# An mLSTM layer in a four-layer kernel: source order for two more engines in its first pass, row work and output norm spread over more chunks

## The chip, the cores and the metric

One core of a Trainium2 chip runs the whole program. Its engines are TensorE (PE, whose weight loads are listed apart as PEld), VectorE (DVE), ScalarE (ACT), GpSimd (POOL) and SyncE (SP); here SP and ScalarE start the DMAs. The metric is the device time of one execution in microseconds (us), lower is better. All times below are us where nothing else is said.

## The reference

Eight images of 32 x 32 positions and 256 channels, in fp32, pass through four residual layers, each `x = x + L_i(groupnorm(x))`. Layers 0, 2 and 3 are attention layers and don't change. Layer 1 is an mLSTM over the 1024 positions of an image, with 8 heads of 64:

```python
up = xs @ W_up.T                                  # 256 -> 1024
x_m, z = up[..., :512], up[..., 512:]
x_act = silu(conv_b + causal_conv4(x_m))          # 4 taps along the sequence
q, k = block_diag(x_act); v = block_diag(x_m)     # 4 x 4 blocks
ig, fg = gates(q, k, v)                           # 8 rows each
lc = cumsum(log_sigmoid(fg))
logD = where(tril, lc_i - lc_j + ig_j, -inf)
m = max_j(logD); D = exp(logD - m)
C = (q @ k.T / 8) * D
h = (C / (max(|sum_j C|, exp(-m)) + 1e-6)) @ v
hn = layernorm_per_head(h) * norm_w
out = ((hn + skip * x_act) * silu(z)) @ W_down.T
```

## The kernel before, in words

All four layers are in one program. Layer 1 is the function `layer1` (from L776). It cuts each image into two segments of 512 tokens, 16 in all, channels on the partitions and tokens in the free dimension, and makes two passes over them.

**First pass** (L1117 to L1160): 64 units u = 4s + c, s the segment and c a quarter of the 512 inner channels. A unit projects `x_m` for its quarter (four matmuls with the z half, `up`, L845), copies it (ScalarE, L864), convolves (ScalarE's tap L871, then three on VectorE, L876) in a bank of PSUM, and takes two Silus (`silu_a` of two units before, L882; `silu_z`, L889). `xm` carries three tokens of the segment before; POOL copies them (L861). When a segment is done its `xm`, `xa` (x_act) and `sz` (silu of z) go to DRAM, and `gates` (L894) makes its gate rows, also for DRAM. In an odd segment the next image's group norm is computed (`norm`, steps stats, mean, scale; `normed` applies it on POOL), the image itself having been asked for one image earlier (`load_x`, on ScalarE's DMA queue).

**Row work** (`rows`, L923 to L1000): for a group of four images, 32 rows (image, head) of 1024 tokens. It is eleven pieces: fetch, soft (|f| and min), soft2 (Exp and Ln, the log-sigmoid), sums (a scan along the row, VectorE), a, most (a second scan), before, within, low, exps (three Exps) and turned (transposes on TensorE into `cols`). Row results that the second pass wants go to DRAM. Group 0's pieces run in the first pass, one a unit from u = 36; group 1's ("late") in the second, at chunks 0, 1, 2, 2, 3, 3, 4, 4, 5, 6 and 7 of their list.

**Second pass** (L1161 to the end): 64 chunks of 128 tokens, four a segment and eight an image; the state is new at each image's first chunk. In chunk n:
- `maxima` (L1045) fetches the row maxima for chunk n+3 into the buffer `d`; `masked` (POOL, L1051) subtracts them from the causal mask for chunk n+2; `decays` (ScalarE, L1056) exponentiates d for chunk n+1 in two halves.
- `scores` (L1176): 8 matmuls into two banks, and VectorE multiplies them into d (L1191).
- for chunk n+1: `queries` (`g`, copied by ScalarE L1077; `gr` = g times the row factor `rb`, VectorE L1080), `keys` (`xt` transposed, weighted into `xaw`, L1092), `value` (`vt`, copied by ScalarE L1106).
- `within` (L1193): the row sums `sums` and the numerators `num_ps`; `across` (L1213) adds the part from the state, then ScalarE evacuates `num_ps` twice (copy L1238, square L1239).
- `update` (L1246): `kv_ps` on TensorE; the old state times its decay on POOL (`decayed`, L1270) and VectorE's sum (L1274, L1276) make the new state.
- Units of the segment before: `spread_rows` (ScalarE's square L1281, `var_ps` L1286, an add on VectorE, ScalarE's Ln L1290 and Exp L1291) in the segment's first chunk; `finish` 0 and 1 (`bc_ps` on TensorE L1297, four operations on VectorE L1301 and L1302, two multiplies on POOL L1305) both in the second; `down` 0 and 1 (L1310, the residual add, the store to DRAM) in the fourth. After the last chunk, four rounds of these remain.

Buffers: the ring of PSUM banks "m" has 4 banks in the first pass (beside 4 for the convolution) and 7 in the second (beside `sums`); every PSUM tile comes from it in turn, so an unread tile holds up the seventh request after it. `d` has four buffers.

**What orders the work.** Inside `manual_schedule` the named engines run their instructions in source order. In the first pass that holds for TensorE and ScalarE; VectorE, POOL and SP are ordered by a scheduler. In the second pass it holds for all but SP. ScalarE's functions come in sets that a table load exchanges; `preload_act_table_set` (L944, L982, L1165) asks for the set that has both Ln and Exp. `start` (L1111) asks for the second pass's first data and masks, at u = 58.

Of the kernel before, what the change touches and what calls it, by code (L numbers as in the profile page):

```python
# [16 lines left out]
P = 128  # L17
# [4 lines left out]
HALF = 512  # L22
# [402 lines left out]
def image_parts(x):  # L425
    return [[x[:, c, hs] for _, hs in halves()] for c in range(2)]
# [349 lines left out]
def layer1(tc, K, src, dst, n_img, a, first):  # L776
# [4 lines left out]
    with tc.tile_pool(name="l1w", bufs=1, reuse_waits="tile") as wk, tc.tile_pool(  # L781
# [41 lines left out]
        def norm(b, step):  # L823
            if step == 0:
                gn.stats(b, image_parts(x[b]))
            elif step == 1:
                gn.mean(b)
            else:
                gn.scale(b)

        def normed(s):
            for c in range(2):
                gn.apply(nc.gpsimd, s // 2, c, seg(s)[:, c], seg(s)[:, c])
# [89 lines left out]
        def rows(i, temp):  # L923
# [18 lines left out]
            def soft2():  # L942
                sp = q["sp"]
                nc.scalar.preload_act_table_set("natural_log_exp_and_others")  # L944
                nc.scalar.activation(sp, sp, AF.Exp, scale=-1.0)
                nc.scalar.activation(sp, sp, AF.Ln, bias=epsn[0:NR, 1:2])
# [34 lines left out]
            def exps():  # L981
                nc.scalar.preload_act_table_set("natural_log_exp_and_others")  # L982
                for k in ("sp", "f", "lc"):
                    nc.scalar.activation(q[k], q[k], AF.Exp)
                nc.sync.dma_start(rowd[i][1], q["sp"])
                nc.sync.dma_start(rowd[i][2], q["lc"])
# [16 lines left out]
        rb, xv, g, gr, xaw, dt, num, sq, nrow = ({} for _ in range(9))  # L1003
# [41 lines left out]
        def maxima(n):  # L1045
            b, t = divmod(n, 2 * NCH)
            dt[n] = wk.tile([P, 4, 2, P], F32, name="d", bufs=4)
            r8 = 8 * (b % GRP)
            r = rowd[b // GRP][0][r8 : r8 + 1, t * P : (t + 1) * P]
            nc.sync.dma_start(dt[n], bass.AP(r.tensor, r.offset, [[0, P], [L, 8], [1, P]]))  # L1050
# [60 lines left out]
        def start():  # L1111

            load_x(0)
            load(0)
            for n in range(3):
                maxima(n)
            masked(0)  # L1117
            masked(1)

        with tc.tile_pool(  # L1120
            name="l1p", bufs=1, space=PSUM, reuse_waits="tile"
        ) as pp, tc.tile_pool(
            name="l1g", bufs=1, space=PSUM, reuse_waits="tile"
        ) as gp, tc.manual_schedule(engines={E.PE, E.Activation}):
            banks["m"] = pp, 4
            if n_img > 1:
                load_x(1, True)
            units = {}
            for i in range(NG - 1):
                todo = rows(i, lambda: wk.tile([P, 2, L], F32, tag="num", name="row", bufs=2))  # L1130
                for k, f in enumerate(todo):
                    units.setdefault(8 * GRP * (i + 1) + 4 + k, []).append(f)
            for u in range(4 * NS + 3):
                s, c = divmod(u, 4)
                if s < NS:
                    b = s // 2 + 1
                    if s % 2 == 0 and c == 0 and s and b < n_img:
                        load_x(b)
                    project(s, c)
                    convolve(s, c)  # L1140
                    if s % 2 and b < n_img and c < 3:
                        norm(b, c)
                    if s % 2 and b < n_img and c == 3:
                        normed(s + 1)
                    if s and s % 2 == 0 and c == 1:
                        normed(s + 1)
                if u >= 2 and u - 2 < 4 * NS:
                    silu_a(*divmod(u - 2, 4))
                if u < 4 * NS:
                    silu_z(s, c)  # L1150
                if NG > 1 and u == 4 * NS - 6:
                    start()
                if NG > 1 and u == 4 * NS + 2:
                    queries(0)
                    keys(0)
                    value(0)
                if c == 2 and s:
                    gates(s - 1)
                for f in units.get(u, []):
                    f()  # L1160
        with tc.tile_pool(  # L1161
# [3 lines left out]
            nc.scalar.preload_act_table_set("natural_log_exp_and_others")  # L1165
            late = rows(NG - 1, lambda: K.big("row"))
            if NG == 1:
                for f in late:
                    f()
                start()  # L1170
                queries(0)
                keys(0)
                value(0)
                late = []
            at = (0, 1, 2, 2, 3, 3, 4, 4, 5, 6, 7)
            late = {n: [f for m, f in zip(at, late) if m == n] for n in range(2 * NCH)}  # L1176
# [68 lines left out]

            def update(n):  # L1246
# [21 lines left out]
                dc = wk.tile([P, 4, 130], F32, name="decayed")  # L1268
                e = rb[s][:, :, t * P + P - 1 : t * P + P].to_broadcast([P, 4, 130])
                nc.gpsimd.tensor_mul(dc, states[n % 2], e)  # L1270
# [8 lines left out]
            def spread_rows(s):  # L1279
                r = nrow[s]  # L1280
                nc.scalar.activation(  # L1281
                    r, r, AF.Square, bias=epsn[:, 0:1], scale=math.sqrt(1e-5)
                )
                ps = ring("var_ps")
                for c in range(4):
                    nc.tensor.matmul(  # L1286
                        ps[32 * c : 32 * c + 32], sel, sq[s][:, c], start=True, stop=True
                    )
                nc.vector.tensor_add(r, r, ps)
                nc.scalar.activation(r, r, AF.Ln)  # L1290
                nc.scalar.activation(r, r, AF.Exp, scale=-0.5)  # L1291

            def finish(s, i):
                ps = [ring("bc_ps") for _ in range(2)]
                for j in range(2):
                    r = slice(64 * i + 32 * j, 64 * i + 32 * j + 32)
                    nc.tensor.matmul(ps[j], bcw[r], nrow[s][r], start=True, stop=True)  # L1297
                for j in range(2):
                    c = 2 * i + j
                    h = num[s, "s"][:, c]  # L1300
                    nc.vector.tensor_mul(ps[j], h, ps[j])  # L1301
                    nc.vector.scalar_tensor_tensor(  # L1302
                        h, xa[s][:, c], par[:, c, 5:6], ps[j], ALU.mult, ALU.add
                    )
                    nc.gpsimd.tensor_mul(h, h, sz[s][:, c])  # L1305

            def down(s, m):
                ps = ring("dn_ps")
                for c in range(4):
                    nc.tensor.matmul(  # L1310
                        ps, wdn[:, c, m * P : (m + 1) * P], num[s, "s"][:, c],
                        start=c == 0, stop=c == 3,
                    )
                nc.vector.tensor_add(seg(s)[:, m], seg(s)[:, m], ps)
                if m == 1:
                    nc.sync.dma_start(dst[:, :, s * HALF : (s + 1) * HALF], seg(s))

            def units(n, k):

                s, t = divmod(n, NCH)  # L1320
                s -= 1
                if s < 0:
                    return
                at = 3 * t + k
                if at == 1:
                    spread_rows(s)
                elif at in (3, 5):
                    finish(s, (at - 3) // 2)
                elif at in (9, 10):
                    down(s, at - 9)  # L1330
# [17 lines left out]
            def prefetch(n):  # L1348
                s, t = divmod(n, NCH)
                if n and n % (2 * NCH) == 0:  # L1350
                    load_x(s // 2)
                if t == 0 and s + 1 < NS:
                    load(s + 1)
                    load_rb(s + 1)
                if t == 3 and s < NS:
                    load_z(s)

            load_rb(0)
            decays(0, range(4))
            for n in range(N):  # L1360
                prefetch(n)
                if n + 3 < N:
                    maxima(n + 3)
# [4 lines left out]
                if n + 1 < N:  # L1368
                    decays(n + 1, (0, 1))
                    keys(n + 1)  # L1370
                    value(n + 1)
                units(n, 1)
# [5 lines left out]
                update(n)  # L1378
                if n + 2 < N:
                    masked(n + 2)  # L1380
                for f in late.get(n, []):
                    f()
                if K.next:
                    follow(N - n)
            for n in range(N, N + NCH):
                for k in range(3):
                    units(n, k)
# [942 lines left out]
```

## Time and profile before

| | us |
|---|---|
| median of 3 runs | 3371.83 (3370.86 to 3379.88) |
| profiled execution | 3368.94 |
| its span | 3367.2 |
| layer 1, first `up` matmul to layer 2's first matmul | 1090.0 to 2026.6 |
| its first pass | 1090.0 to 1370.2 |
| its second pass, image 0 | 1370.2 to 1462.4 |
| its second pass, the other images | 1462.4 to 1998.5 |
| from the last scores to layer 2 | 1998.5 to 2026.6 |
| mean granted clock of TensorE in the span | 0.974 |

The trace shows an engine's instructions in groups: start, duration, engine and line, the operation, out<-in by the program's names, partitions x elements, count. Brackets at the end are the idle time of the engine in front of the group and what ended it. `ACT_TABLE_LOAD` is ScalarE's change of table set. The granted clock is a share of full speed.

Matmul records of the layer's largest groups: `up_ps` x512 takes 232.4, `dn_ps` 116.4, `num_ps` 75.3 for the part inside the chunk and 62.6 from the state, `sc` 74.4, `g_ps` 74.0, `vt_ps` 68.6. On ScalarE `decays` (L1062) takes 164.0 in 512 instructions of 392 ns; on POOL `masked` 152.4 in 64 of 2386 ns; on VectorE d times scores 81.9 in 128 of 681 ns.

### The profile page before, as it was taken

The numbers are of one execution on the slowest core, as the hardware profiler recorded it, in microseconds if no ns is written. First come the engines' busy times: TensorE is split into PE (matmuls) and PEld (weight loads), VectorE is DVE, ScalarE is ACT, GpSimd is POOL, SyncE is SP. The second block draws the span as 40 slices with busy tenths as digits, with TensorE's granted clock in tenths as the row PEclk, the third lists the DMA queues.
The fourth block names the chain that finished last, engine by engine and source line by source line (L and its number), as shares of the span: only waits on it lengthen the run. The fifth ranks groups of instructions, "written<-read, shape, count | busy, mean of one in ns | idle before, by whom it ended". The sixth has DMA issues, their size and how long they took to land.

```text
span 3367.2 us, 77570 instructions
## 1 busy us (share of the span) xinstructions
PE 3206.9 (95%) x30760; PEld 1646.7 (49%) x30760; DVE 2177.8 (65%) x5559; ACT 2247.9 (67%) x5040; POOL 1490.2 (44%) x1069
## 2 busy tenths in 40 slices
PE   7999999999998998899999989999998999999997
PEld 3323323323222444666666755666664555555554
DVE  4776776776675666555555565666665667777775
ACT  3666666766666668554554446667776788889885
POOL 4233233223321011244444445343435667888777
PEclk9999999999999999999999999999999779999999
DMA  3000000000001666767777733111111001111001
GB/s 139 14 26 1 26 26 1 26 17 11 26 7 39 240 225 217 231 182 181 195 194 184 211 91 101 46 58 52 40 49 48 14 14 33 32 34 39 27 27 61
DMA packets 138911, 268.00 MB, mean 80 GB/s; under 512 B 9202, under 2 KB 77172, under 8 KB 130228
## 3 DMA queue, kind: packets, MB, share of 16 engines
q1 hardware_dynamic: 132164, 242.67, 23.7%
q10 hardware_dynamic: 6384, 20.37, 1.9%
q8 instruction: 243, 3.98, 0.5%
q14 instruction: 120, 0.98, 0.1%
HBM read 177.81 MB, written 85.20 MB: 78 GB/s over the span
## 4 chain that ended last, share of the span: by engine, by line
PE 71%; ACT 9%; DVE 6%; POOL 6%; issue 4%; DMA 3%; POOLq 0%; ACTq 0%; SPq 0%; DVEq 0%
PE s L675 7%; PE sm L693 6%; PE num L720 6%; PE qkv_ps L1763 5%; PE qkv_ps L1982 4%; PE dn_ps L1310 3%; PE up_ps L849 3%; PE qk_ps L550 3%; PE pt L1545 3%; PE pt L1673 2%; PE fac_ps L2084 2%; ACT e L2043 2%; PE o_ps L603 2%; PE pr_ps L1823 2%; PE o L1564 2%
## 5 line engine op out<-in xcount | busy, mean ns | idle before, releaser
L681 DVE TENSOR_TENSOR e<-s,ret 128x1024 f32<-128x1024 f32 x512 | 602.9, 1219 | 180.5 <-PE s L675 176.5
L685 ACT ACTIVATE ea<-e 128x1024 f32<-128x1024 f32 x512 | 535.1, 1054 | 268.1 <-DVE e L681 234.1
L675 PE MATMUL s<-qk,qk 32*128 32x512 f32 x2048 | 300.5, 640 | 2.4 <-POOL qk L567 1.7
L1531 POOL TENSOR_TENSOR e<-e,su 128x616 f32<-128x616 f32 (+2 forms) x128 | 157.3, 1229 | 270.3 <-DVE su L1530 239.2
L693 PE MATMUL sm<-ea,ones 128*32 128x512 f32 x2048 | 273.0, 604 | 2.0 <-DVE dn L701 2.0
L720 PE MATMUL num<-e,v 128*32 128x512 f32 x2048 | 266.6, 592 | 0.0
L1678 DVE COPY pts<-pt 112x512 f32<-112x512 f32 x256 | 175.9, 687 | 133.9 <-PE pt L1673 132.4
L2043 ACT ACTIVATE e<-win,disc 128x196 f32<-128x196 f32 x512 | 239.6, 544 | 0.2
L849 PE MATMUL up_ps<-x,wup 128*128 128x512 f32 x512 | 232.4, 606 | 4.8 <-ACT sz L889 2.3
L1663 POOL TENSOR_TENSOR e<-e,su 128x784 f32<-128x784 f32 x128 | 191.4, 1495 | 87.1 <-DVE su L1662 59.8
L1655 ACT ACTIVATE e<-e,mx 128x196 f32<-128x196 f32 x512 | 228.0, 453 | 0.0
L2050 POOL TENSOR_TENSOR e<-e,win 128x784 f32<-128x784 f32 x128 | 201.8, 1577 | 38.1 <-issue 31.5
L1526 ACT ACTIVATE e<-e,mx 128x154 f32<-128x154 f32 (+2 forms) x512 | 212.1, 425 | 0.0
L1053 POOL TENSOR_TENSOR d<-cmask,d 128x1024 f32<-128x1024 f32 x64 | 152.4, 2386 | 105.7 <-DMA d<-l1rows 105.7
L1982 PE MATMUL qkv_ps<-xq,w 128*128 128x512 f32 x384 | 192.0, 627 | 1.2 <-ACT fac L2077 1.2
L1062 ACT ACTIVATE d<-d,cols 128x128 f32<-128x128 f32 x512 | 164.0, 392 | 43.3 <-POOL d L1053 43.2
L1763 PE MATMUL qkv_ps<-x,w 128*128 128x512 f32 x384 | 181.3, 609 | 1.6 <-POOL x L236 1.6
L1673 PEld LDWEIGHTS pt<-idg,e 128*112 128x112 f32 x1024 | 120.5, 139 | 121.1 <-issue 89.9
L675 PEld LDWEIGHTS s<-qk,qk 32*128 32x128 f32 x2048 | 85.3, 183 | 184.2 <-issue 119.1
L1305 POOL TENSOR_TENSOR num<-num,sz 128x512 f32<-128x512 f32 x64 | 81.4, 1272 | 207.6 <-ACT vt L1106 109.6
L1673 PE MATMUL pt<-idg,e 128*112 128x128 f32 x1024 | 165.1, 287 | 8.4 <-DVE oT L1697 3.1
L876 DVE SCALAR_TENSOR_TENSOR cv<-xm,par,cv 128x512 f32<-128x512 f32 x192 | 140.7, 750 | 47.0 <-ACT cv L871 44.1
(243 smaller groups left out, 6711.7 us busy)
## 6 DMA issues: line engine op xcount, KB each, us to landing
d<-l1rows SPq DMA_DIRECT2D x64, 512.0 KB
x<-x SPq DMA_DIRECT2D x25, 1024.0 KB
x<-x SPq DMA_DIRECT2D x32, 512.0 KB
l1xm<-xm SPq DMA_DIRECT2D x16, 1024.0 KB
l1sz<-sz SPq DMA_DIRECT2D x16, 1024.0 KB
xv<-l1xm SPq DMA_DIRECT2D x32, 512.0 KB
l1xa<-xa SPq DMA_DIRECT2D x16, 1024.0 KB
xa<-l1xa SPq DMA_DIRECT2D x16, 1024.0 KB
```

The lines of the kernel that those rows point to most:

```text
L675: nc.tensor.matmul(s[:, j % 2], qk[b, 1, c][g, kb * P : (kb + 1) * P], qk[b, 0, c][g, h * HALF : (h + 1) * HALF], start=True, stop=True,)
L681: nc.vector.tensor_mul(e[n, i], s, m)
L685: nc.scalar.activation(ea[n, i], e[n, i], AF.Abs)
L693: nc.tensor.matmul(acc["sm"][g, :], ones, ea[n, j // 2][:, j % 2, :], start=kb == 0, stop=kb == 7,)
L720: nc.tensor.matmul(acc["num"][g, :], v[b][:, kb, vc], e[n, j // 2][:, j % 2, :], start=kb == 0, stop=kb == 7,)
L849: nc.tensor.matmul(ps, wup[:, kc, m * P : (m + 1) * P], seg(s)[:, kc], start=kc == 0, stop=kc == 1,)
L1526: self.nc.scalar.activation(p[:, j], p[:, j], AF.Exp, scale=-1.0, bias=mx[:, j : j + 1], accum_out=su[:, j : j + 1],)
L1655: self.nc.scalar.activation(e[:, j], e[:, j], AF.Exp, scale=-1.0, bias=mx[:, j : j + 1], accum_out=self.su[:, j : j + 1],)
L1673: self.nc.tensor.transpose(ps[: self.PART, at : at + P], self.tile(n)[:, 2 * i + j, k * self.PART : (k + 1) * self.PART], self.K.ident,)
L1763: nc.tensor.matmul(ps, w[:, kc, o : o + P], x[b][:, kc, h * HALF : (h + 1) * HALF], start=kc == 0, stop=kc == 1,)
L1982: nc.tensor.matmul(ps, w[:, kc, o : o + P], xq[b][:, kc, h * HALF : (h + 1) * HALF], start=kc == 0, stop=kc == 1,)
L2043: nc.scalar.activation(e[:, j], win[:, 0], AF.Tanh, scale=disc[b][:, i, 8 + h : 9 + h], bias=disc[b][:, i, h : h + 1],)
```

## The change

It changes `layer1` alone.

1. In the first pass VectorE and POOL join TensorE and ScalarE in source order. The group norm's steps are placed by unit: for image b (first unit 8b) a quarter of `stats` in each of the units 8b−10 to 8b−7, `mean` at 8b−5, `root` at 8b−4, the two halves of `normed` at 8b−2 and 8b+1. Images from 2 on are asked for at 8b−16, two images ahead; every third has its own buffer.
2. Group 0's row pieces stand at u = 36 + (0, 2, 4, 5, 7, 8, 10, 12, 14, 16, 18). The late ones stand at chunks 0, 3, 4, ... 12, one a chunk, in front of `units(n, 1)` and `within`, where they stood at the chunk's end. The late pieces no longer ask for a table set; one request stands at the second pass's start, as before.
3. `start` stays at u = 58 without its masks; `load_rb(0)` moves from the second pass to u = 63, and the masks of chunks 0 and 1 to u = 63 and 65. `maxima` runs four chunks ahead, with five buffers for d.
4. `decayed` for chunk n+1 is computed at the end of chunk n, in front of `masked(n+2)` (`decay`).
5. Output norm: `squared` and `spread_rows` in the segment's first chunk, `finish` 0 in the second, `finish` 1 in the third, `down` in the fourth. The last segment goes in two halves of 256 tokens.
6. The second pass's `load_x` moves from an image's first chunk to its sixth, from the second image on.

```diff
-        ) as gp, tc.manual_schedule(engines={E.PE, E.Activation}):
+        ) as gp, tc.manual_schedule(engines={E.PE, E.Activation, E.DVE, E.Pool}):
...
+            for b in range(1, n_img):
+                u = 8 * b
+                if b > 1:
+                    at(u - 16, load_x, b, b % 3 == 1)
+                for i in range(4):
+                    at(max(u - 10, 1) + i, lambda b=b, i=i: gn.stats(b, image_parts(x[b]), i))
+                at(max(u - 5, 5), gn.mean, b)
+                at(max(u - 4, 6), gn.root, b)
+                at(max(u - 2, 7), normed, 2 * b)
+                at(u + 1, normed, 2 * b + 1)
...
-                for k, f in enumerate(todo):
-                    units.setdefault(8 * GRP * (i + 1) + 4 + k, []).append(f)
+                for k, f in zip((0, 2, 4, 5, 7, 8, 10, 12, 14, 16, 18), todo):
+                    at(8 * GRP * (i + 1) + 4 + k, f)
+            if NG > 1:
+                at(4 * NS - 6, start)
+                at(4 * NS - 1, load_rb, 0)
+                for i in range(2):
+                    at(4 * NS - 1 + 2 * i, masked, i)
+                for f in (queries, keys, value):
+                    at(4 * NS + 2, f, 0)
...
-            nc.scalar.preload_act_table_set("natural_log_exp_and_others")
-            late = rows(NG - 1, lambda: K.big("row"))
+            log_exp()
+            late = rows(NG - 1, lambda: K.big("row"), lambda: None)
...
-            at = (0, 1, 2, 2, 3, 3, 4, 4, 5, 6, 7)
-            late = {n: [f for m, f in zip(at, late) if m == n] for n in range(2 * NCH)}
+            late = dict(zip((0, 3, 4, 5, 6, 7, 8, 9, 10, 11, 12), late))
...
+            def decay(n):
+
+                if 0 < n % (2 * NCH) < 2 * NCH - 1:
+                    s, t = n // NCH, n % NCH
+                    decayed[n] = wk.tile([P, 4, 130], F32, name="decayed")
+                    e = rb[s][:, :, t * P + P - 1 : t * P + P].to_broadcast([P, 4, 130])
+                    nc.gpsimd.tensor_mul(decayed[n], states[n % 2], e)
...
+            for s in range(NS - 1):
+                n, w = NCH * (s + 1), slice(0, HALF)
+                at(n, 0, squared, s, w)
+                at(n, 1, spread_rows, s, w)
+                at(n + 1, 0, finish, s, 0, w)
+                at(n + 2, 0, finish, s, 1, w)
+                at(n + 3, 0, down, s, 0, w)
+                at(n + 3, 1, down, s, 1, w)
+            s, w = NS - 1, [slice(0, 2 * P), slice(2 * P, HALF)]
+            at(N - 2, 1, squared, s, w[0])
+            at(N - 2, 2, spread_rows, s, w[0])
+            at(N - 1, 2, finish, s, 0, w[0])
+            for f, *args in (
+                (squared, w[1]), (finish, 1, w[0]), (spread_rows, w[1]),
+                (down, 0, w[0]), (down, 1, w[0]), (finish, 0, w[1]), (finish, 1, w[1]),
+                (down, 0, w[1]), (down, 1, w[1]),
+            ):
+                at(N, 0, f, s, *args)
...
-                if n and n % (2 * NCH) == 0:
+                if n > 2 * NCH and n % (2 * NCH) == 5:
                     load_x(s // 2)
...
-            load_rb(0)
             decays(0, range(4))
             for n in range(N):
+                if n + 4 < N:
+                    maxima(n + 4)
                 prefetch(n)
-                if n + 3 < N:
-                    maxima(n + 3)
                 scores(n)
...
+                if n in late:
+                    late[n]()
                 units(n, 1)
                 within(n)
...
                 update(n)
+                decay(n + 1)
                 if n + 2 < N:
                     masked(n + 2)
-                for f in late.get(n, []):
-                    f()
```

## The prediction

> **What bounds the kernel now.** I read the page first (busy shares, then the chain that ended last), then the layer's four stages in the table of windows, then the groups of each engine inside one segment.
>
> ```profile
> PE 3206.9 (95%) x30760; PEld 1646.7 (49%) x30760; DVE 2177.8 (65%) x5559; ACT 2247.9 (67%) x5040; POOL 1490.2 (44%) x1069
> ...
> PE 71%; ACT 9%; DVE 6%; POOL 6%; issue 4%; DMA 3%; POOLq 0%; ACTq 0%; SPq 0%; DVEq 0%
> ```
>
> TensorE is busy 95% of the span and carries 71% of the chain. The changed layer can only win back TensorE's idle time, and the half-speed stretches that such idle time leaves behind. The stages of the layer (us; then busy time of PE, PEld, DVE, ACT, POOL; clock; DMA share):
>
> ```profile
> 1090.00:1370.20 280.20, 266.12 (x1601) 129.81 (x1599) 178.28 (x314) 188.59 (x293) 35.32 (x53) 0.98 0.65 234
> 1370.20:1462.40 92.20, 73.74 (x868) 56.69 (x868) 48.02 (x78) 47.78 (x108) 33.80 (x18) 0.89 0.73 193
> 1462.40:1998.50 536.10, 509.17 (x6088) 371.61 (x6087) 307.46 (x569) 273.38 (x701) 238.17 (x152) 0.99 0.69 180
> ```
>
> They are the first pass, the head of the second pass (chunks 0 to 7, image 0) and its other 56 chunks. Against each I set what TensorE alone needs.
>
> First pass: a clean segment (1330.18 to 1346.18) takes 15.85 of matmuls, so 16 take 254; seven group-norm steps at 0.5, the column transposes 1.1 and the last 2.3 make 260. It takes 280: **20 are lost**.
>
> Head: two clean segments are 63.85. It takes 92.2: **28.4 lost**, at a clock of 0.89.
>
> Rest: a clean segment is 36.5 where an image's first half is computed (no state yet) and 37.25 where its second half is, so 14 make 503.5 with the longer `sums`. It takes 536: **32.5 lost**. The lost time has a face here, VectorE's line of the same chunk first:
>
> ```profile
> 1599.07 0.85 DVE L1274 TENSOR_TENSOR state<-decayed,kv_ps 64x256 f32<-64x256 f32 x2 [1.61 <-POOL decayed L1270]
> ```
> ```profile
> 1600.84 0.94 PE L1204 MATMUL sums<-d,hot 128*32 128x128 f32 x16 [2.03 <-DVE d L1191]
> 1601.71 1.98 PE L1210 MATMUL num_ps<-d,vt 128*64 128x128 f32 x16
> ```
>
> Brackets hold the wait before a group and what ended it. Once a segment, in its third chunk, TensorE waits for `d*scores`; that is late because the chunk before gave VectorE two `finish` (8 operations, 5.8) and put their four POOL multiplies ahead of `decayed`, which the state add waits for. In four of seven cases the 2.03 wait is followed by half-speed matmuls (1.98, where the same group took 1.09 ten us earlier); every other segment waits 1.59, and is never slow after it.
>
> **Part 1, decay a chunk ahead and `finish` in two chunks.** No work is added (POOL 1.06, four VectorE operations 2.9, only moved). `decayed(n+1)` follows chunk n's state add, and each chunk has one `finish`. VectorE's largest chunk load falls by 2.9, more than the 2.03 wait, so the 14 stalls (25.9 with their small variation), the half-speed matmuls (about 1.6 in four segments) and most of the longer `sums` go: 32.5 if nothing comes in their place. `masked(n+2)` now stands behind `decayed` on POOL, whose 1.06 is costed below.
>
> **Part 2, a new cost on ScalarE.** The late row pieces no longer request the set that holds both Ln and Exp, and the remaining request ends, in the built order, at the program's very start. The second pass then runs on separate sets: each segment's Ln and Exp (of `nrow`) need a load each, 34 loads where there were 3. The trace prices one:
>
> ```profile
> 1299.07 1.28 ACT L1062 ACT_TABLE_LOAD   x1
> 1300.36 0.40 ACT L1062 ACTIVATE d<-d,cols 128x128 f32<-128x128 f32 x1
> ```
>
> 1.28 a load, and the next ACTIVATE starts 0.01 after its end. The Trainium skill, "ScalarE: Activation LUTs", "What ACT_TABLE_LOAD costs", gives 1283 ns plus a drain of 1380 ns, 2.66 a switch. By the rule 34 loads are 90 and a pair is 5.3; by the rows 43.6 and 2.57. I take the rows. ScalarE is busy only 273 of 536, so the sum of loads costs nothing by itself; the place does:
>
> ```profile
> 1583.02 0.72 ACT L1281 ACTIVATE nrow<-nrow,epsn 128x512 f32<-128x512 f32 x1
> 1584.49 0.63 ACT L1290 ACTIVATE nrow<-nrow 128x512 f32<-128x512 f32 x1 [0.75 <-DVE nrow L1289]
> 1585.15 0.63 ACT L1291 ACTIVATE nrow<-nrow 128x512 f32<-128x512 f32 x1
> 1585.69 1.26 ACT L1062 ACTIVATE d<-d,cols 128x128 f32<-128x128 f32 x4
> 1586.86 0.56 ACT L1238 COPY num<-num_ps 128x512 f32<-128x512 f32 x1
> 1587.32 0.59 ACT L1239 ACTIVATE sq<-num_ps 128x512 f32<-128x512 f32 x1
> ```
>
> This is a segment's first chunk; its first score matmul began at T = 1578.54. ScalarE's order stays: behind Ln and Exp stand four decays and the two evacuations of `num_ps`. `squared` ends at T+5.1 (its wait for VectorE then falls inside the first load); load, Ln, load, Exp add 1.28 + 0.63 + 1.28 + 0.63: `nrow` is ready at T+8.95. Four decays and two evacuations (2.2 with their overlaps) free the bank of `num_ps` at T+11.15. TensorE, in a chunk without state (6.44 of matmuls, then the next scores 1.09 and queries 1.09), wants `nrow` for the broadcast `bc` at T+8.62: 0.35 to 0.4 of wait. After it come `bc` 1.06 and `xt` 0.44, and `vt`, the seventh bank on, wants `num_ps`' own at T+10.5: 0.65. Together 1.05. With state, `decayed` puts the mask later on POOL (state at T+1.3, 1.06, mask 2.35: T+4.85), the decays behind it wait, and the chain moves by 1.4: 0.45 at `bc`, 1.15 at `xt`: 1.6. Seven of each: 18.6. Bounds: zero if the loads are wholly covered, 14 x 2.57 = 36 if nothing covers it, plus 1.6 in each segment whose wait reaches the 2.0 after which matmuls ran at half speed. Here the skill ("TensorE: Matmul & The Clock Gate", Part 1, the HAM clock gate) puts the fall at an idle window of about 3.4. By that rule no wait here would slow anything; by the rows a 2.03 wait did in four of seven. I keep the rows: waits of 1.05 and 1.6 stay under it. Gain of parts 1 and 2 together: 32.5 − 18.6 = **14** (−10 to 30).
>
> **Part 3, head.** Two things make it: `rb` (11.18 on VectorE, 5.59 on TensorE) and the row pieces, several to a chunk (TensorE waits 3.77 and, 34 later, 5.42).
>
> ```profile
> 1383.87 0.69 DVE L1080 TENSOR_TENSOR gr<-g_ps,rb 128x512 f32<-128x512 f32 x1 [11.18 <-DMA rb<-l1rows]
> ```
> ```profile
> 1407.89 1.16 PE L1204 MATMUL sums<-d,hot 128*32 128x128 f32 x16 [3.77 <-DVE d L1191]
> ```
>
> `load_rb(0)` is asked for five units earlier, but it reuses an `xm` buffer and stands on SP's queue behind the last segment's stores, which the last `silu_z` releases about when the second pass begins: 0 to 4 remain. One piece a chunk, the longest a scan of 2.3 to 3.0 on VectorE, fits the 8 of a chunk where pairs (two scans and row steps of 1.2) did not. Left: a load and two activations on ScalarE in chunk 3 or 4 (about 4, and 1.5 of slow clock), `rb` 3, small ones 1.5: 10 in place of 28.4. Gain **18** (12 to 24). The row fetch's DMAs go ahead of the fifth `d` on SP's queue; that is in the low end.
>
> **Part 4, first pass.** POOL and VectorE follow the source, and the masks move from u=58 to u=63 and 65.
>
> ```profile
> 1275.09 2.34 POOL L1053 TENSOR_TENSOR d<-cmask,d 128x1024 f32<-128x1024 f32 x1 [25.31 <-DMA d<-l1rows]
> ...
> 1277.61 0.78 ACT L871 ACTIVATE cv<-xm,par 128x512 f32<-128x512 f32 x1 [5.86 <-POOL xm L861]
> ```
>
> POOL waited 25.31 for a DMA with the `xm` halo copy queued behind it; TensorE then idled 5.5 and ran at 0.8 to 0.9 clock, 7 in all. With the mask five units later this goes. What else was lost is eight decays of chunk 0 set among Silus: 16 loads, 20.5 of ScalarE at 5.25 a unit where TensorE needs 4.1, 9 with the clock. After, eight loads remain (units 60 to 63: ScalarE 21.3, TensorE 15.6): 6, and 2 for the clock at the very end, where `gates(15)` and the first `g` wait. Rows spread over more units and group-norm quarters save 1 to 3. From 20 lost to 10: gain **10** (5 to 14). Images loaded two ahead: their tiles arrived with no wait that the trace shows, 0 (0 to 1).
>
> **Part 5, tail by halves.** TensorE waits 0.85, 2.20 and 2.95 in the last 28, but layer 2 is held elsewhere:
>
> ```profile
> 2017.73 8.97 PE L1310 MATMUL dn_ps<-num,wdn 128*128 128x512 f32 x16 [2.95 <-POOL num L1305]
> ...
> 2020.52 12.17 ACTq L1737 DMA_DIRECT2D bias<-l_rpb  x8
> ```
>
> Its bias DMAs occupy ScalarE's queue to 2032.7. Four loads for two halves come in, 5.1, beside a ScalarE that is busy 3.7 of the 28. I take 0 (−3 to +2). The second pass's `load_x` at the sixth chunk instead of the first waits for nothing that I find: 0.
>
> Sum: 10 + 18 + 14 + 0 = 42. The profiled execution took 3368.94, its span 3367.2; 3368.94 − 42 = 3327. The median, 3371.83, lies 2.9 above: **3330**.
>
> **Rivals.**
> A, as above: 3330, chance 0.52, its own range 3317 to 3345.
> B, the loads eat all that part 1 brings: stalls of 2.3 a segment (14 x 2.3 = 32). For it: all of ScalarE's chain in that chunk is serial. Against: it has 3 to 5 of slack in the rows above. Gain 10 + 18 = 28: 3344. Chance 0.18.
> C, the loads are covered and nothing replaces the stalls: 10 + 20 + 32 + 8 of tail and first pass = 70: 3302. For it: only 51% ScalarE busy; against: the order is fixed, so no other work fills in. Chance 0.14.
> D, slower: each pair lands whole on the path. If `bc`, `xt` and `vt` stop TensorE for 2.57 or more, it passes the 2.03 from which half-speed matmuls followed, +1.8: 4.4 x 14 = 61 against 32.5, so 29 lost; the 18 of the head and the 10 of the first pass are needed to make it even. Slower begins where the head and first pass give under 19 beside it, as when `rb` and the row fetch stay late: 29 − 10 = 19 lost, 3391. Against: it needs the clock to fall in every segment. Chance 0.08.
> E, the change doesn't do what it says: Silu and Exp still alternate at the first pass's end, and "one request at the start" holds no set. If the gains are cancelled there, within 10: 3370. Chance 0.08.
>
> **How the numbers follow.** Measurement tells this kernel from no change at about 0.3%, 10 us. Faster by more: A, B, C, 0.84; same: E, 0.08; slower: D, 0.08. The range leaves out D, most of E, and the far half of C: 3300 to 3364.
>
> **What would show it.** Right: no 25 wait of POOL before the halo copy; no `sums` wait on `d` in each third chunk; table loads at the Ln and Exp of `nrow`, 1.28 each, 2.57 a segment; waits of 0.4 to 1.6 at `bc`, `xt` or `vt` on ScalarE; eight loads at the end of the first pass; chunks 1 to 7 under 10. Wrong: waits of 2 and more at `bc` with clock under 0.95 in steady segments (B, D); no wait there at all (C); a head as long as before, with VectorE on `rb`.

## The result and the profile after

The changed kernel takes 3333.88 (median of 4 runs, 3328.35 to 3341.76) beside 3372.01 for the kernel before: a ratio of 0.9886, 95% interval 0.9869 to 0.9903, or 38 us less. Its profiled execution took 3334.75, its span is 3333.0. From layer 2's first matmul to the end the profiles take 1340.6 and 1340.7, so the 34.2 between the two spans lies in layer 1.

Stages of the changed kernel in the table of windows (us; busy time of PE, PEld, DVE, ACT, POOL; clock; DMA share; GB/s):

```profile
1089.60:1366.40 276.80, 266.70 (x1601) 131.74 (x1599) 184.96 (x314) 178.44 (x285) 35.86 (x52) 0.98 0.67 239
1366.40:1437.00 70.60, 66.59 (x854) 52.12 (x852) 42.52 (x73) 43.11 (x104) 30.89 (x18) 0.95 0.74 204
1437.00:1966.90 529.90, 512.26 (x6113) 374.15 (x6109) 312.69 (x575) 313.10 (x735) 241.09 (x153) 0.99 0.74 187
```

| stage | before | after | gain | forecast |
|---|---|---|---|---|
| first pass, from the first `up` at 1089.85 and 1089.61 | 280.4 | 276.8 | 3.6 | 10 |
| image 0 of the second pass | 92.2 | 70.6 | 21.6 | 18 |
| its other images | 536.0 | 529.9 | 6.1 | 14 |
| last scores to layer 2 | 28.1 | 25.4 | 2.7 | 0 |

ScalarE's busy time in the third stage rose from 273.4 to 313.1; 29 table loads of 1.28 make 37.2 of it. The old wait of `sums` for `d` is gone; its place is taken by this (ScalarE, then TensorE, in an image's second half):

```profile
1638.05 1.28 ACT L1303 ACT_TABLE_LOAD   x1
1639.35 0.63 ACT L1303 ACTIVATE nrow<-nrow 128x512 f32<-128x512 f32 x1
1639.99 1.28 ACT L1304 ACT_TABLE_LOAD   x1
1641.29 0.63 ACT L1304 ACTIVATE nrow<-nrow 128x512 f32<-128x512 f32 x1
```
```profile
1641.97 1.13 PE L1310 MATMUL bc_ps<-nrow,bcw 32*128 32x512 f32 x4 [0.54 <-ACT nrow L1304]
1644.10 0.66 PE L1085 MATMUL xt_ps<-idg,xa 128*128 128x128 f32 x4 [1.00 <-ACT sq L1242]
```

Each Ln and Exp brings its load, and the Exp's end releases `bc`. The copies of `num_ps` come out late behind it and hold `xt`. In an image's first half it is `bc` and `vt`, 0.8 to 0.9.

Two places of the first pass explain most of what it still loses, image 1's normalization and the last units:

```profile
1126.61 5.83 PE L843 MATMUL up_ps<-x,wup 128*128 128x512 f32 x9 [3.20 <-POOL x L236]
...
1360.37 0.65 PE L894 MATMUL gate_ps<-xa,gw 128*32 128x128 f32 x8 [3.47 <-ACT xa L876]
```

The first of them follows from VectorE's order: the shift of image 1 (L230) stands behind unit 7's convolution (L870), which had to wait itself.

```profile
1123.16 2.34 DVE L870 SCALAR_TENSOR_TENSOR cv<-xm,par,cv 128x512 f32<-128x512 f32 x3 [2.50 <-ACT cv L865]
1125.41 0.33 DVE L230 TENSOR_SCALAR gn<-gn 128x1 f32<-128x1 f32 x2
```

From 1110 to 1130 the clock was 0.83 to 0.84, from 1360 to 1370 0.71. In image 0 of the second pass one chunk of eight still stands out, chunk 5 with 14.57 (8.1 without a wait; chunk 7 takes 13.2 in every image, since `down` stands there):

```profile
1407.17 2.08 PE L1310 MATMUL bc_ps<-nrow,bcw 32*128 32x512 f32 x4 [3.41 <-ACT nrow L1304]
1409.18 1.11 PE L1085 MATMUL xt_ps<-idg,xa 128*128 128x128 f32 x4
1410.09 1.91 PE L1099 MATMUL vt_ps<-bdv,xv 128*128 128x128 f32 x8
```

The same four `bc` matmuls take 1.13 elsewhere; after the wait they ran at half speed.

### The profile page after: what moved, and what is told of

The parts are those of the page before. It is cut to its first block, busy times and chain, and to the rows that moved or that the text cites. A ratio compares the mean times of both kernels' runs of the same rounds, so it can differ in the third digit from the quotient of the medians.

```text
span 3333.0 us, 77642 instructions
## 1 busy us (share of the span) xinstructions
PE 3203.6 (96%) x30792; PEld 1649.6 (49%) x30792; DVE 2185.0 (66%) x5570; ACT 2277.6 (68%) x5066; POOL 1491.7 (45%) x1073
## 5 line engine op out<-in xcount | busy, mean ns | idle before, releaser
L1696 POOL TENSOR_TENSOR e<-e,su 128x784 f32<-128x784 f32 x128 | 191.3, 1495 | 82.7 <-DVE su L1695 53.9
L870 DVE SCALAR_TENSOR_TENSOR cv<-xm,par,cv 128x512 f32<-128x512 f32 x192 | 144.7, 754 | 85.5 <-ACT cv L865 80.9
L1255 POOL TENSOR_TENSOR decayed<-state,rb 128x520 f32<-128x520 f32 x48 | 50.8, 1058 | 304.7 <-PE sc L1188 112.5
L1678 DVE CUSTOM_DVE_ANT_0 e<-s,e 128x196 f32<-128x196 f32 x512 | 153.7, 357 | 8.0 <-PE s L1665 4.2
```

## The experiments

The layers around layer 1 differ by up to 12 between profiles of unchanged code, as much as some effects here. So each run is also read by its stages, and in the second pass by chunks: a chunk's time is the difference between the starts of its `sc` matmuls and the next chunk's. An image is eight chunks; in the changed kernel images 2 to 6 take 76.2 each, in the kernel before 77.6 to 79.3. Where no engine is named, numbers are TensorE's.

**The shared table set kept (e_set).** In the changed kernel:

```diff
-            late = rows(NG - 1, lambda: K.big("row"), lambda: None)
+            late = rows(NG - 1, lambda: K.big("row"), log_exp)
```

> The changed kernel with the late row pieces asking for the shared set of Ln and Exp again; from chunk 4 on no table is exchanged, 34 loads become 2. Theory (what is left of the steady stall is the two loads in front of the output norm's Exp): the waits of TensorE for ScalarE at bc, xt and vt in the second pass (12.6 in the 57 chunks from 10 on) go to under 2, an image of eight chunks takes 73.8 instead of 76.2, chunk 5 loses a load of its stall (14.6 to about 10 to 12), and the kernel gains 17 to 20 on the changed one (about 3315). Rival (the stall comes from the mask that now stands behind the decay on GpSimd, the loads are covered): the images stay within 0.5 of 76.2 and the gain is under 5.

Measured: 3306.24 (ratio to before 0.9795, 0.9776 to 0.9814). The other images:

```profile
1435.30:1940.90 505.60, 504.07 (x6114) 370.48 (x6114) 313.71 (x576) 277.49 (x710) 241.61 (x153) 1.00 0.76 196
```

TensorE is busy 504.07 of 505.60 at full clock; most images take 73.36. Against 529.9 that is 24.4, more than expected. The half-speed stretches went as well, and 3.4 of it is chunk 10, most of that a stop of TensorE for which the profile shows no cause (see e_rows below); without it 21 are left. Chunk 5 fell to 12.6 only: soft2's own two activations and one load still stand in front of Ln. The rival is refuted: without the loads, decay and mask in their new order cost nothing.

**The same loads in the kernel before (e_loads).** There the late pieces' two requests are left out and nothing else is changed:

```diff
-                nc.scalar.preload_act_table_set("natural_log_exp_and_others")
+                if table:
+                    nc.scalar.preload_act_table_set("natural_log_exp_and_others")
...
-            late = rows(NG - 1, lambda: K.big("row"))
+            late = rows(NG - 1, lambda: K.big("row"), False)
```

> The kernel before with one thing taken over from the change: its late row pieces no longer ask for the shared set of Ln and Exp, so that each segment's Ln and Exp exchange tables. Theory (the loads in front of nrow's Exp come onto the path by themselves, whatever the order of decay and finish): TensorE's waits for ScalarE at bc, xt and vt appear here too, 1.0 to 1.6 a segment, 14 to 22 in all, an image of eight chunks takes 80 to 81 instead of 77.6 to 79.3, and the kernel is 10 to 20 slower than before. Rival (the two loads fit into the time that the segment's stall leaves anyway): within 5 of before.

Measured: 3396.32, ratio 1.0069 (1.0046 to 1.0093); the other images 560.1 instead of 536.0, an image 81.1 to 82.7. The loss, 21 by the medians, is a little more than the 10 to 20 expected, and its place was another. TensorE's waits there, window 1460 to 1960 (waits, total, times, longest):

```profile
PE sums L1206 <- DVE d L1193: 30.5, 12, 2.6
PE bc_ps L1299 <- ACT nrow L1293: 2.6, 6, 0.4
```

The late ScalarE made the old stall longer, 2.64 instead of 1.59 in an image's first half and 2.45 instead of 2.03 in its second, and the clock of this stage fell to 0.97. So the loads cost about as much in either kernel: 24 here, 21 to 24 in the changed one.

**Finish in one chunk again, and the decay at its old place,** each with the shared set kept (s_norm1, s_olddec):

```diff
-                at(n + 2, 0, finish, s, 1, w)
+                at(n + 1, 2, finish, s, 1, w)
```

> The changed kernel with the shared set kept (as in e_set, an image of eight chunks 73.4) and both finishes in one chunk again, the decay still a chunk ahead. Theory (the old stall in a segment's third chunk was VectorE's eight finish operations and then its wait for the decay on GpSimd, 1.6 of the 2.0): with the decay ahead 0 to 0.5 of the stall comes back a segment, an image takes 73.4 to 74.4. Rival (the finish alone overfilled VectorE): the stall comes back whole, an image takes 76.5 to 77.6.

```diff
-                update(n)
-                decay(n + 1)
+                decay(n)
+                update(n)
```

> The changed kernel with the shared set kept (as in e_set, an image of eight chunks 73.4) and the decay at its old place, in the chunk that uses it, behind the finish's multiplies on GpSimd; the finish in two chunks. Theory (with one finish a chunk the multiplies are done 2.6 earlier, so the decay is in time): an image takes 73.4 to 74.4, so that either part alone would have removed the stall. Rival (the decay behind any multiply is late): a stall of 1 to 2 in each chunk with a finish, an image takes 76 to 80.

Measured: an image takes 74.24 with both finishes in one chunk (3322.09, ratio 0.9847, 0.9820 to 0.9873), and 73.36 with the old decay (3309.15, ratio 0.9807, 0.9783 to 0.9832), where one image took 76.0 by a single late chunk. In that chunk, 54, the rival did appear: the decay stood behind late multiplies, VectorE waited for it, and TensorE waited 1.31 for VectorE.

```profile
1863.34 0.85 DVE L1283 TENSOR_TENSOR state<-decayed,kv_ps 64x256 f32<-64x256 f32 x2 [1.01 <-POOL decayed L1255]
```

Either part alone takes nearly all of the old stall. The finish split takes it whole but for that one chunk; the decay ahead would guard against it, and adds nothing else that the chunk times show.

**Decay and mask exchanged (e_swap),** in the changed kernel with its loads:

```diff
                 update(n)
-                decay(n + 1)
                 if n + 2 < N:
                     masked(n + 2)
+                decay(n + 1)
```

> The changed kernel with the two GpSimd steps at a chunk's end exchanged: the mask of chunk n+2 in front of the decay for chunk n+1. Theory (where there is a state, the decay in front of the mask moved ScalarE's chain by 1.4 and made the waits of an image's second half 1.6 instead of 1.05): the waits at bc and xt of the second half fall to those of the first, its second chunk from 9.8 to 9.3, about 3.5 in all (7 segments by 0.5); the decay, 2.4 later, is in time with one finish a chunk. Rival (the decay is now late): VectorE's state add waits and chunks with a finish take 1 or more longer, 14 and more in all.

Measured: 3315.41, ratio 0.9840 (0.9823 to 0.9856); the other images 513.6. TensorE's waits, window 1470 to 1930:

```profile
PE bc_ps L1310 <- ACT nrow L1304: 2.6, 6, 0.4
PE vt_ps L1099 <- ACT sq L1242: 2.5, 6, 0.4
PE xt_ps L1085 <- ACT sq L1242: 0.8, 5, 0.2
```

The first half's waits stay as they were. The second half's fall from 1.54 to 0.2, its second chunk from 9.8 to 8.37: the whole 1.4 of the shift, not the half of it that was expected, since that chunk has more matmuls in front of `bc` than the first half's. The rest of the 16 is chunk 61, 14.0 to 9.4, most of whose half-speed matmuls went with the waits, and chunk 10, 12.9 to 8.7. Chunk 10 is not the exchange's: with the old order it takes 8.66 too wherever its stop stays away (see e_rows). Without it 12 of the 16 are left, about half of what the loads cost in these images; with the shared set the order costs nothing.

Image 0 shows the order as well. In the changed kernel ScalarE sat idle in chunk 4, in front of soft2, until the mask behind the decay was ready:

```profile
1399.49 1.28 ACT L1059 ACTIVATE d<-d,cols 128x128 f32<-128x128 f32 x4 [2.22 <-POOL d L1050]
```

Here that wait is gone, and chunk 5 takes 8.13 instead of 14.57 with the same loads and the same soft2; a stop of 1.16 in chunk 4 gave ScalarE some of that time. Image 0 takes 66.4 instead of 70.6.

**The late row pieces away from the finishes (e_rows):** slots 0, 2, 3, 3, 7, 7, 11, 11, 15, 15, 19, and an own buffer for image 1.

> The changed kernel with the late row pieces at chunks 0, 2, 3, 3, 7, 7, 11, 11, 15, 15 and 19, that is never in a chunk that has a finish or the output norm's ScalarE chain; image 1 gets its own buffer in the second pass so that the rows can hold theirs longer. Theory (a row piece of 1.9 to 3.0 on VectorE beside a finish of 2.9 overfills a chunk, and soft2 beside Ln and Exp overfills ScalarE): chunk 5 falls from 14.6 to 9.8, chunk 10 from 12.9 to 8.1, together 9.5 less, about 3325. Rival (chunk 10 is late because its d arrives late by DMA behind the row fetch): chunk 10 stays over 11, gain 5.

Measured: 3333.95, ratio 0.9882 (0.9859 to 0.9904), no gain. Chunk 10 fell to 8.14 as expected, but that does not show that the row piece had made it late. In the changed kernel, with the piece beside the finish, TensorE waits only 0.29 for VectorE there. What follows is a stop in the middle of a group, and half speed behind it; `<-issue` says that the profile shows nothing that TensorE waited for:

```profile
1456.47 1.13 PE L1099 MATMUL vt_ps<-bdv,xv 128*128 128x128 f32 x8 [0.29 <-DVE state L1285]
1458.11 1.09 PE L1213 MATMUL num_ps<-d,vt 128*64 128x128 f32 x15
1461.70 0.48 PE L1213 MATMUL num_ps<-d,vt 128*64 128x128 f32 x1 [2.50 <-issue]
```

In e_exp0 and e_mask58 (below) chunk 10 has the same instructions, the stop doesn't come, and the chunk takes 8.66. In e_exp0 every engine keeps the changed kernel's times within 0.02 up to that point, and then:

```profile
1453.07 1.09 PE L1215 MATMUL num_ps<-d,vt 128*64 128x128 f32 x16
```

So the row piece costs 0.5 of chunk 10, and the other 4.2 is the stop, whose cause is open. And chunks 4 and 5 took 11.6 and 13.2: here the scan stood in the same chunk as soft2, and VectorE waited for it with all else behind it:

```profile
1397.27 2.28 DVE L946 TENSOR_TENSOR_SCAN row<-row 32x1024 f32<-32x1024 f32 x1 [6.35 <-ACT row L943]
```

**Image 1's shift a unit earlier (e_img1), and chunk 0's decays behind the last Silu (e_exp0):**

```diff
-                at(max(u - 2, 7), normed, 2 * b)
+                at(max(u - 2, 6), normed, 2 * b)
```

> The changed kernel with the first half of image 1's normed one unit earlier (u = 6, right behind root), so that its shift on VectorE does not stand behind unit 7's convolution. Theory: TensorE's 3.2 wait for x on GpSimd at 1126.6 goes, and with it the slow clock after it: the first pass takes 271 to 273 instead of 276.9, about 3330. Rival (image 1's data arrive late by DMA): the wait stays, first pass 276 to 277.

```diff
-                for f in (queries, keys, value):
-                    at(4 * NS + 2, f, 0)
+                at(4 * NS + 2, queries, 0)
+                at(4 * NS + 2, decays, 0, range(4))
+                at(4 * NS + 2, keys, 0)
+                at(4 * NS + 2, value, 0)
...
-            decays(0, range(4))
+            if NG == 1:
+                decays(0, range(4))
```

> The changed kernel with the decays of chunk 0 behind the first pass's last Silu instead of among the Silus. Theory (Silu and Exp exchange tables five times in the last four units, ScalarE becomes the bound there and the last gates wait): ten loads become two, the waits of gate_ps for ScalarE (4.8) go, and with the half-speed matmuls behind them the first pass takes 270 to 272 instead of 276.9, about 3329. Rival (the wait only moves to the first score product, which needs all eight decays of chunk 0): first pass plus chunk 0 within 2 of 282.4.

Measured: first pass 271.1 and 270.6 instead of 276.8, each 6 less, as expected of the first and at the good end of the second. In e_exp0 11 loads became 3; chunks 0 and 1 took 6.05 and 7.55 instead of 5.57 and 6.93, so 1.1 of the wait moved there and the rest went. As wholes they took 3335.70 (0.9881, 0.9860 to 0.9902) and 3326.98 (0.9851, 0.9826 to 0.9875); in the first the gain drowned in slow-clock chunks and in the spread of the other layers.

**The masks of chunks 0 and 1 back at u = 58 (e_mask58):** in the changed kernel, `at(4 * NS - 6, masked, i)`; one run.

> The changed kernel with the masks of chunks 0 and 1 back at u = 58, where start asks for their data. Theory (before, GpSimd waited 25 for a mask's DMA with the halo copy of xm behind it; moving the mask removed that): GpSimd again waits about 20 in front of the mask, the convolution waits 4 to 6 for xm, TensorE idles as much, and the first pass takes 281 to 285 instead of 276.9. Rival (source order on GpSimd alone had cured it, or the data now come earlier): within 1 of 276.9.

Measured: 3334.01, first pass 283.6. The size is what I expected and the cause is not. GpSimd did not wait for the mask at all:

```profile
1324.47 4.65 POOL L1050 TENSOR_TENSOR d<-cmask,d 128x1024 f32<-128x1024 f32 x2
```

What came back was the alternation of Exp and Silu. With the mask ready early, the decays of chunk 0 find room among eight units instead of four, and 18 loads stand where there were 11 (1280 to 1374):

```profile
L876 ACT ACT_TABLE_LOAD x9 | 11.5, 1283 | 0.2
L1059 ACT ACT_TABLE_LOAD x8 | 10.3, 1283 | 0.1
L918 ACT ACT_TABLE_LOAD x1 | 1.3, 1283 | 0.0
```

So the rest of the first pass's change cures GpSimd's wait of 25, without the mask's move; that it is source order on GpSimd, which puts the mask behind other work, is likely but was not tried alone. The later mask saves table loads.

**The last segment whole (e_whole),** as before:

> The changed kernel with the last segment whole, as before. Theory (the halves bring the end of layer 1 forward; what the profile showed in chunk 61 has nothing to do with them): from the last scores to layer 2 27 to 29 instead of 25.4, chunk 61 stays at 12 to 14, the time 2 to 4 longer, not to be told apart from the changed kernel. Rival (the halves' extra ScalarE and table work makes chunk 61 late): chunk 61 falls to 9.8, and the tail gives that back.

Measured: 3338.88, ratio 0.9907 (0.9890 to 0.9923). From the last scores to layer 2 30.8 instead of 25.4; chunks 56 to 62 are 2.3 shorter, so the halves bring about 3 net, or nearly 5 if chunk 61 is left out. It stayed at 12.5, so they are not what delays it; with them it takes 12.4 to 14.0 in five profiles.

**All findings together (e_best, e_best2).** First with image 1 asked for at chunk 13, then at chunk 6 (the second shown; both have the first pass's two edits as well):

```diff
+                at(4 * NS + 2, log_exp)
                 at(4 * NS + 2, decays, 0, range(4))
...
-            late = rows(NG - 1, lambda: K.big("row"), lambda: None)
+            late = rows(NG - 1, lambda: K.big("row"), log_exp)
...
-            late = dict(zip((0, 3, 4, 5, 6, 7, 8, 9, 10, 11, 12), late))
+            slots = (0, 3, 7, 11, 11, 15, 15, 19, 19, 19, 23)
+            late = {n: [f for m, f in zip(slots, late) if m == n] for n in slots}
...
+                if n == 6:
+                    load_x(1, True)
+                if n > 4 * NCH and n % (2 * NCH) == 5:
```

> The changed kernel with what the runs so far found: the shared set of Ln and Exp kept from the end of the first pass on; the decays of chunk 0 behind the last Silu; the first half of image 1's normed a unit earlier; the late row pieces at chunks 0, 3, 7, 11, 11, 15, 15, 19, 19, 19 and 23, where no finish runs, with an own buffer for image 1 in the second pass. If the gains add: first pass 265 (276.9 less 6 less 6), image 0 65 to 67 (70.6 less the 6 of chunk 5), the chunks from 8 to 63 502 to 504 (529.9), together about 45 less than the changed kernel: 3288. If the soft2 and scan pieces only find another chunk to overfill: 3295 to 3300.

> e_best with the second pass's image 1 asked for at chunk 6 instead of 13, where its request stood on ScalarE's queue for 7.9 behind another load of the same DMA lane and took 8.2 from chunks 13 and 14. Theory: those chunks fall from 24.4 to 15.9 and the kernel to about 3291 to 3294; all else as in e_best (first pass 263.7, chunks 0 to 7 66.7). Rival (the request stands on ScalarE's queue at chunk 6 as well): chunks 6 and 7 take the same 8 longer.

Measured: 3300.96 (ratio 0.9783, 0.9757 to 0.9810), then 3295.10 (0.9779, 0.9764 to 0.9793). The first is 13 behind the sum of the gains, the second 1 behind its range. In the first, chunks 13 and 14 took 24.4. In its trace ScalarE's queue shows why: the request for image 1 was issued late, and `g`, behind it, came 7.9 late.

```profile
1473.86 0.53 ACTq L795 DMA_DIRECT2D x<-x  x1
1474.43 0.59 ACT L1074 COPY g<-g_ps 128x512 f32<-128x512 f32 x1 [7.87 <-DMA sz<-l1sz]
```

The request waited on the semaphore of the transfer of `sz`, which SP had asked for at 1453.10; both carry the same one. Asked for at chunk 6, it cost nothing there, and chunks 13 and 14 took 16.0. The three stages of the second version:

```profile
1090.00:1353.90 263.90, 260.77 (x1601) 128.98 (x1601) 184.85 (x314) 165.19 (x269) 35.98 (x52) 1.00 0.69 247
1353.90:1421.70 67.80, 65.67 (x853) 51.70 (x852) 36.07 (x70) 44.80 (x112) 30.06 (x18) 0.97 0.81 231
1421.70:1925.50 503.80, 503.32 (x6112) 370.33 (x6108) 318.67 (x578) 277.49 (x709) 241.84 (x153) 1.00 0.78 197
```

In the third TensorE idles 0.5 of 503.8. This version beats both kernels; what it still has to gain in these stages, against the 260 and 63.85 that TensorE alone needs, is about 4 in each of the first two.

## Why the prediction was right, and where it was off

The forecast was 3330; 3333.88 was measured. The direction, the total and the main mechanism held; the terms did not all. Between the two profiled executions, which the terms were taken from, the gain is 34 against the 42 of the sum: two terms fell short by 14, two exceeded theirs by 6. That the medians lie 38 apart and so close to the forecast is in part luck.

- **Old stall (part 1): right.** It went whole. The forecast took both parts for it; s_norm1 and s_olddec show that either suffices. It also said that the 2.03 wait was followed by slow matmuls in four of seven cases; by chunk times (10.2 to 10.5 instead of 8.9) it is three of six, and the seventh wait was 1.78. The 503.5 that TensorE alone needs in this stage are not 14 whole segments, which would be 516: the stage ends with the last scores, a chunk short. As a figure it held (e_best2: 503.8).
- **Loads (part 2): right in mechanism, place and base size.** The rows' 1.28 a load holds: the next ACTIVATE starts 0.01 to 0.02 after its end. Waits of 1.05 and 1.6 a segment were worked out; about 0.85 and 1.54 came, and images 2 to 6 lose 76.2 − 73.36 = 2.9 each, 20 for seven, where the sum had 18.6. What was missed is 4 to 5 more: the mid stage lost 24.4 against e_set. Chunk 61 (half speed behind waits of 0.2 and 1.0) and chunk 10 are its bulk. The one was costed at nothing because waits under 2.03 were said not to slow the clock; the other is the stop of 2.50, which no load explains and which no place of the kernel before shows.
- **That clock step failed.** In chunks 21, 29, 37, 45 and 53 of six profiles the pair of waits 0.54 and 1.00 stands 24 times. Half speed followed in none of 4 in the changed kernel, 2 of 4 in e_img1, 1 of 4 in e_exp0, 3 of 5 in e_mask58, none of 4 in e_rows and none of 3 in e_whole. In the kernel before, a wait of 2.40 (chunk 58) was not followed by it either, where 2.02 was. The same waits, the same code: the length of a single wait does not decide it. How much of the changed kernel's spread of 13 comes from this is not shown, since one execution of it was traced.
- **Head (part 3): right in kind, the size a little low.** 21.6 against 18. The 3 for `rb` was not needed: VectorE shows no wait for it. Of the 10 left, 6.7 came, nearly all in chunk 5, where soft2, Ln, Exp and two loads follow each other on ScalarE, as forecast for chunk 3 or 4. Chunk 5 was said to stay under 10. What the sum lacked is the mask behind the decay: it had been costed for the steady segments, but in chunk 4 it kept ScalarE idle for 2.22 in front of all this, and with the mask first (e_swap) the stall is gone.
- **First pass (part 4): the step that was off.** The end of it came as forecast: waits of 4.8 and about 2 of slow clock for 6 and 2, though nine loads stand among the Silus, not eight. But source order had been costed at a gain only. For image 1 it brought waits of 4.9 from 1110 to 1130, where TensorE had none before: 1.71 for the statistics and 3.20 for the shift behind unit 7's convolution; and 2.5 of slow clock. e_img1 takes back the 3.20 and the clock behind it, 5.7 in all; 3.6 + 5.7 is nearly the 10 that had been forecast. The 1.71 stays in e_img1. And the reason given for the gain was in part wrong: the mask's move cut table loads (e_mask58, one run), it did not free GpSimd.
- **Tail (part 5): wrong, by 2.7.** Layer 2's bias transfers had been taken for what holds it; they moved forward together with layer 1's end (1989.17, 3.1 before layer 2's first matmul in place of 6.0), so they do not hold layer 2: something at layer 1's end lets them go. The halves are worth 3 to 5.
- **Rivals.** B's stalls of 2.3 did not come; C's 3302 is near what e_set gives with the loads taken away (3306), though C had put 8 in the first pass and the tail. D's mechanism is near what e_loads shows: where the loads meet the old order, the kernel gets slower. E's alternation of Silu and Exp did remain, at about the cost that part 4 had put there.

## What to carry to other kernels

When a change moves a request for a function table, count the loads in the built order and cost each at the place where it stands, not by ScalarE's idle time: on an engine that was half idle they cost 21 to 24, in waits of one microsecond, beside the 38 that the change brought net. A step that is moved earlier can let others slip in behind it, as the early mask let Exps in among Silus, so look at what it releases. Of two cures for one stall, test each alone: here the split of the finish was all but enough, and the order that the other cure set on GpSimd cost something elsewhere.

## What the runs showed that was not expected

Equal waits (0.54 and 1.00, with 1.1 of matmuls between them) were followed by matmuls at half speed in 6 of 24 cases and not in the others; a wait of 1.59 never was, 2.03 in three of six. TensorE can stop in the middle of a group for nothing that the profile shows: in chunk 10 for 2.50 in the changed kernel, 2.48 in e_whole, 1.58 in s_olddec, 0.98 in e_set, 0.44 in e_img1 and not at all in e_exp0, e_mask58 and e_swap, always in front of the last one or two matmuls of the same group. The kernel before and e_loads have no such stop in layer 1. A DMA request on ScalarE's queue stood 7.9 for a transfer of other data that had been asked for on SP, and ScalarE's computations stood behind it. One row scan of 32 x 1024 took 2.28 where GpSimd stood still and 2.98 where GpSimd's multiply ran beside its first 0.8; what made the difference was not tried.
